# Cross attention: the scores of each head's last 16 rows on eight TensorE tiles instead of four

## The chip, the cores and the metric

The kernel runs on one core of a Trainium2 chip. The metric is the time of one execution on the device in microseconds; lower is better. TensorE does the matmuls and writes PSUM, ScalarE (ACT) and VectorE (DVE) read PSUM and work on SBUF, GpSimd (POOL) works on SBUF, and SyncE (SP) issues most DMAs.

## The reference

Sixteen sequences of 100 rows and 640 columns (`hidden_states`) attend to 718 context rows of 384 columns, with 8 heads of 80. A second, small attention by way of four more tokens is added. All in float32. The part that matters here is the first attention's scores:

```python
query = hidden_states @ Wq                     # 16 x 100 x 640
keyt = enc @ Wk                                # 16 x 718 x 640
valt = enc @ Wv
hs = _mha(query, keyt, valt)                   # softmax(q k^T / sqrt(80)) v, 8 heads of 80
...                                            # ca_hs2: the attention by way of the tokens
out = (hs + ca_hs2) @ Wout + b_out + residual
```

## The kernel before

The loop over the 16 batches is unrolled, and within it each engine's instructions run in the order in which the program issues them (a manual schedule). A batch `b` goes through these steps on TensorE: the scores of its queries against its keys in three groups (`scores(b, 0)`, `scores(b, 1)`, `scores(b, 2)`, L593), the products of the second attention (L823, L771), the values of this batch and the keys of the next in turns (L433 and L464), the last keys (L558), sometimes an output projection (L1048) or queries (L534), and then the weighted sums of the values (`a_ps`, L1453), after which the next batch begins with its scores.

The 718 keys are cut in six blocks of 120 or 119 (`KN` = 120). A group of scores takes two of them (`a` = 0, 1). Scores stand transposed: keys on the partitions, the 800 rows of the 8 heads along the free dimension, in four PSUM banks `s_ps[0..3]`, each with two heads' rows for both key blocks. A head has 80 columns, and so 80 rows of contraction, which don't fit into 64 partitions. They are cut into the first 64 and the last 16:

- `first_rows` (L618) contracts the first 64. Two heads lie above one another in 128 partitions, so there are two row groups of 64 partitions, and the 120 keys are cut into column tiles of 64 and 56 by `KH = [(0, 64), (64, KN)]` (L69). The moving operand is one head's 100 rows. A group of scores has 32 such products.
- `last_rows` (L637) contracts the last 16. All eight heads' last rows lie together in one chunk of 128 partitions (`kT[:, 4]`), two heads to 32 partitions. `qz` holds the queries for it, masked so that each of the two heads meets only its own 16: the moving operand is 200 elements, the 100 rows of the one head and then of the other. There are four row groups of 32 partitions (`RG` = 4), each writes a bank of its own, and each takes all 120 keys in one product. A group of scores has 8 such products.

Both write through the helper `product` (L605), so that all have line L608 in the profile; they are told apart by their inputs, `qp` and `qz`, and by their shapes. `product` adds to what the bank holds, and begins anew the first time that a quadrant of 32 partitions of a bank is written. Group 1 runs `last_rows` ahead of `first_rows`, groups 0 and 2 the other way round, so that the steps of groups 0 and 1 and those of groups 1 and 2 that have the same tiles lie next to each other:

```python
        steps = (last_rows, first_rows) if g == 1 else (first_rows, last_rows)
```

After a group, ScalarE copies the four banks to SBUF (L664 for groups 0 and 2, two banks at a time; L658 for group 1). Groups 0 and 2 use the same banks (`pair`), group 1 others.

Of the kernel before, what the change touches and what calls it, by code (L numbers as in the profile page):

```python
# [14 lines left out]
B, S, H = 16, 100, 640  # L15
# [8 lines left out]
KN = KT // 2  # L24
# [44 lines left out]
KH = [(0, 64), (64, KN)]  # L69
# [57 lines left out]
def kernel(  # L127
# [33 lines left out]
    def pair(name):  # L161
        tile = ps2.tile([P, 2, 512], F32, tag="ps2", name=name)
        return tile
# [21 lines left out]
    def scores_tile(name):  # L185
        return main.tile([P, 2, ROWS], F32, tag="st", name=name, bufs=NP)
# [28 lines left out]
    def load_enc(b):  # L215
        enc = enc_tile(f"enc_{b}"), None
        for u, lo, hi in ((0, 0, 3), (1, 1, 3), (2, 0, 2)):
            at = A_RAW[u, lo]
            nc.sync.dma_start(
                out=enc[0][:, at : at + hi - lo],  # L220
                in_=enct[b][:, lo:hi, u * (KT - 1) : u * (KT - 1) + KT],
            )
        return enc

    def load_rest(b, enc):
        if b == 1:
            room = hsT_tile("rest_1").rearrange("p c s -> p (c s)")
            rest = room[:, : len(A_REST) * KT].rearrange("p (i k) -> p i k", k=KT)
        else:
            rest = rest_tile(f"rest_{b}")  # L230
        for (u, c), i in A_REST.items():
            nc.sync.dma_start(
                out=rest[:, i], in_=enct[b][:, c, u * (KT - 1) : u * (KT - 1) + KT]
            )
        return enc[0], rest
# [19 lines left out]
    kT = const.tile([P, HC, 3, KT], F32, name="kT")  # L255
# [337 lines left out]
    def scores(b, g, tiles):  # L593

        qp, qz = tiles
        name = f"s_ps_{b}_{g}"
        if g == 1:
            s_ps = [f(f"{name}_{r}") for r, f in enumerate((psumk, psumk, psum1, psum1))]
        else:
            pairs = [pair(f"{name}_{i}") for i in range(2)]  # L600
            s_ps = [pairs[r // 2][:, r % 2] for r in range(RG)]
        n = KN
        begun = set()

        def product(at, part, w, rhs, cols, last):  # L605

            k0, k1 = part
            nc.tensor.matmul(  # L608
                s_ps[at][k0:k1, cols],
                w,  # L610
                rhs,
                start=not begun & {(at, k) for k in range(k0, k1, 32)},
                stop=last,
                skip_group_check=True,
            )
            begun.update((at, k) for k in range(k0, k1, 32))

        def first_rows(last):  # L618

            for a in range(2):  # L620
                u, j = KC[2 * g + a]
                for c in range(RG):
                    rhs = qp[:, c // 2, c % 2, (b % 2) * S : (b % 2 + 1) * S]
                    for r in range(2):
                        h, rows = RG * r + c, slice(64 * r, 64 * r + 64)
                        lo = 256 * a + (h % 2) * S
                        for k0, k1 in KH:
                            product(
                                h // 2,
                                (k0, k1),  # L630
                                kT[rows, c, u, j * KN + k0 : j * KN + k1],
                                rhs[rows],
                                slice(lo, lo + S),
                                last,
                            )

        def last_rows(last):  # L637

            for a in range(2):
                u, j = KC[2 * g + a]  # L640
                for r in range(RG):
                    rows = slice(32 * r, 32 * r + 32)
                    product(
                        r,
                        (0, n),
                        kT[rows, 4, u, j * KN : (j + 1) * KN],
                        qz[rows, 0, b % 2],
                        slice(256 * a, 256 * a + 2 * S),
                        last,
                    )  # L650

        steps = (last_rows, first_rows) if g == 1 else (first_rows, last_rows)
        for i, step in enumerate(steps):
            step(i == 1)
        st = scores_tile(f"st_{b}_{g}")[:n]
        if g == 1:
            for r in range(RG):
                nc.scalar.copy(  # L658
                    st[:, :, 2 * r * S : 2 * (r + 1) * S],
                    s_ps[r][:n].rearrange("p (a q) -> p a q", a=2)[:, :, : 2 * S],  # L660
                )
        else:
            for i in range(2):
                nc.scalar.copy(  # L664
                    st[:, :, 4 * i * S : 4 * (i + 1) * S].rearrange(
                        "p a (r q) -> p r a q", r=2
                    ),
                    pairs[i][:n].rearrange("p r (a q) -> p r a q", a=2)[:, :, :, : 2 * S],
                )
        return st  # L670
# [554 lines left out]
    last, enc_next, second_next = None, load_rest(1, load_enc(1)), Second(1, xT)  # L1225
# [8 lines left out]
    for b in range(B):  # L1234
# [243 lines left out]
        last = mine  # L1478
# [55 lines left out]
```

## Time and profile before

| what | value |
|---|---|
| median of the runs | 926.78 us (925.39 to 928.07, 3 runs) |
| profiled execution | 925.19 us |
| span of its instructions | 923.5 us |
| TensorE busy | 916.1 us, 99% of the span |
| VectorE, GpSimd, ScalarE busy | 687.4, 685.2, 434.0 us |
| granted TensorE clock | 0.999 |
| scores (L608), share of the chain that ended last | 11% |

A line of a group's view reads: line, engine, operation, tiles out<-in, shape, number of records, then the time in which at least one of them ran, the mean duration of one, and the idle time of the engine ahead of them. A shape such as `32*120 32x200` is 32 rows by 120 columns of the array and a moving operand of 32 partitions by 200 elements. PE is the matmuls, PEld the loads of the stationary operand into the array. An f32 product shows as two records of each.

### The profile page before, as it was taken

How to read it: one execution, taken by the hardware profiler on the slowest of the kernel's cores; microseconds unless marked ns; L12 is line 12 of the kernel's file. 1: busy time of each engine (PE TensorE's matmuls, PEld its weight loads, DVE VectorE, ACT ScalarE, POOL GpSimd, SP SyncE). 2: the span in 40 equal slices, each digit the busy share in tenths (PEclk: the TensorE clock that was granted, in tenths of full speed). 3: DMA queues.
4: the chain of work that ended last, by engine and by line, in shares of the span. 5: the costliest groups of instructions: out<-in, count | busy, mean ns of one | idle time of the engine just before them, and what ended most of it. 6: DMA issues, size and time to landing. Idle time of an engine off the chain costs nothing.

```text
span 923.5 us, 25899 instructions
## 1 busy us (share of the span) xinstructions
PE 916.1 (99%) x11130; PEld 773.0 (84%) x11130; DVE 687.4 (74%) x1085; ACT 434.0 (47%) x836; POOL 685.2 (74%) x646
## 2 busy tenths in 40 slices
PE   9999999999999999999999999999999999999998
PEld 6987889788797879888798887988879888797866
DVE  3459895988738897795867869579783898838883
ACT  2234543737327463552636526264641737427341
POOL 5757999688947888497784968758996589956723
PEclk9999999999999999999999999999999999999999
DMA  8822013050300404031030311205031050310201
GB/s 263 266 85 78 25 49 93 2 156 2 103 31 13 116 2 132 3 99 59 19 114 3 111 46 30 76 2 155 2 92 41 2 155 2 103 45 2 82 20 40
DMA packets 49673, 62.82 MB, mean 68 GB/s; under 512 B 14072, under 2 KB 38200, under 8 KB 49560
## 3 DMA queue, kind: packets, MB, share of 16 engines
q1 hardware_dynamic: 45512, 51.49, 18.1%
q0 software_dynamic: 3024, 8.53, 3.0%
q8 instruction: 87, 1.43, 0.6%
q10 hardware_dynamic: 1024, 1.15, 0.4%
q14 instruction: 26, 0.21, 0.1%
HBM read 55.59 MB, written 5.57 MB: 66 GB/s over the span
## 4 chain that ended last, share of the span: by engine, by line
PE 96%; DVE 2%; DMA 0%; issue 0%; ACT 0%; POOL 0%; ACTq 0%; DVEq 0%
PE a_ps L1453 12%; PE s_ps L608 11%; PE v_psA L433 11%; PE v_psB L433 9%; PE kT_ps L558 8%; PE k_psA L464 8%; PE q_ps L534 7%; PE k_psB L464 6%; PE o_ps L1048 5%; PE v_psC L433 3%; PE k_psC L464 3%; PE v_psD L433 2%; PE v_psE L433 2%; PE y_ps L771 2%; PE v_ps L374 1%; PE k_psE L464 1%
## 5 line engine op out<-in xcount | busy, mean ns | idle before, releaser
L796 POOL TENSOR_TENSOR e<-ca,g 100x800 f32<-100x800 f32 x64 | 97.9, 1540 | 115.5 <-PE v_psB L433 101.5
L499 POOL TENSOR_TENSOR enc<-enc 128x240 f32<-128x240 f32 x135 | 111.0, 832 | 16.5 <-DMA enc<-in_enct 9.4
L1256 DVE TENSOR_TENSOR st<-st,over 120x1600 f32<-120x1600 f32 x48 | 118.1, 2463 | 0.0
L1453 PEld LDWEIGHTS a_ps<-vs,st 120*36 120x36 f32 (+3 forms) x3072 | 109.2, 125 | 4.9 <-issue 4.8
L1453 PE MATMUL a_ps<-vs,st 120*36 120x81 f32 (+3 forms) x3072 | 112.0, 233 | 0.0
L433 PE MATMUL v_psA<-wv_sb,enc 128*120 128x320 f32 x352 | 109.8, 434 | 0.0
L897 POOL TENSOR_TENSOR hs<-hs,hs 100x640 f32<-100x640 f32 x48 | 102.0, 2125 | 3.8
L664 ACT COPY st<-s_ps 120x800 f32<-120x800 f32 x64 | 49.7, 829 | 98.7 <-PE s_ps L608 98.7
L803 POOL TENSOR_TENSOR e<-e,e 100x800 f32<-100x800 f32 x48 | 92.7, 1932 | 3.8
L890 POOL TENSOR_TENSOR hs<-vb,p 100x640 f32<-100x640 f32 x64 | 87.9, 1383 | 9.4 <-issue 4.8
L433 PE MATMUL v_psB<-wv_sb,enc 128*120 128x320 f32 x296 | 91.8, 433 | 0.0
L1264 ACT ACTIVATE st<-st 120x1600 f32<-120x1600 f32 x48 | 73.8, 1538 | 33.5 <-DVE st L1256 33.4
L464 PE MATMUL k_psA<-enc,wk_sb 128*128 128x240 f32 x360 | 87.8, 367 | 1.1 <-DVE kT L404 1.1
L464 PEld LDWEIGHTS k_psA<-enc,wk_sb 128*128 128x128 f32 x360 | 68.2, 190 | 18.4 <-POOL e L796 1.6
L1268 DVE TENSOR_TENSOR most<-most,st 120x800 f32<-120x800 f32 x64 | 71.2, 1113 | 15.6 <-ACT st L658 14.4
L433 PEld LDWEIGHTS v_psA<-wv_sb,enc 128*120 128x120 f32 x352 | 63.2, 183 | 22.6 <-issue 0.5
L464 PE MATMUL k_psB<-enc,wk_sb 128*128 128x240 f32 x300 | 73.1, 366 | 0.3 <-DVE sm L873 0.3
L608 PE MATMUL s_ps<-qp,kT 64*56 64x100 f32 (+1 forms) x3072 | 73.1, 248 | 0.0
L433 PEld LDWEIGHTS v_psB<-wv_sb,enc 128*120 128x120 f32 x296 | 54.1, 183 | 21.9 <-DVE vs L404 0.4
L608 PEld LDWEIGHTS s_ps<-qp,kT 64*56 64x56 f32 (+1 forms) x3072 | 66.9, 130 | 5.6 <-issue 4.2
L963 ACT COPY hsT<-turned_hs 32x160 f32<-32x160 f32 (+7 forms) x244 | 67.7, 278 | 3.0
L534 PE MATMUL q_ps<-xT,wq_sb 128*128 128x200 f32 x400 | 69.1, 333 | 0.0
(168 smaller groups left out, 1789.3 us busy)
## 6 DMA issues: line engine op xcount, KB each, us to landing
vb<-va_d POOLq DMA_DIRECT2D x32, 250.0 KB, 3.7
vb<-va_d SPq DMA_DIRECT2D x32, 250.0 KB
enc<-in_enct SPq DMA_DIRECT2D x30, 240.0 KB
enc<-in_enct SPq DMA_DIRECT2D x15, 360.0 KB
xT<-in_xt SPq DMA_DIRECT2D x8, 500.0 KB
rest<-in_enct SPq DMA_DIRECT2D x31, 120.0 KB
xn<-in_x SPq DMA_DIRECT2D x11, 320.0 KB
out<-xn SPq DMA_DIRECT2D x11, 320.0 KB
```

The source lines that it names most:

```text
L433: nc.tensor.matmul(at[0][j][:KN, : H // 2], a_form(self.enc, f)[:, j * KN : (j + 1) * KN], wv_there.get(f, wv_sb[:, W_AT[f]]), start=first ...
L464: nc.tensor.matmul(at[:, i * KT : (i + 1) * KT], wk_sb[:, W_AT[f], i], a_form(self.enc, f), start=(first and i == 0), stop=last, skip_grou ...
L499: nc.gpsimd.tensor_tensor(out, left, right, op)
L534: nc.tensor.matmul(q_ps[:, : 2 * S].rearrange("p (j s) -> p j s", j=2), wq_sb[:, c, n * P : (n + 1) * P], xT[:, :, c, :], start=(c == 0), ...
L558: nc.tensor.matmul(bank[:, i * KT : (i + 1) * KT], weights[c], a_raw(enc, u, c), start=(i == 0 and c == 0), stop=(c == CC - 1), skip_group ...
L608: nc.tensor.matmul(s_ps[at][k0:k1, cols], w, rhs, start=not begun & {(at, k) for k in range(k0, k1, 32)}, stop=last, skip_group_check=True,)
L796: first = nc.gpsimd.tensor_tensor(to, self.ca[:, t, :].unsqueeze(1).to_broadcast([S, NH, S]), g[:, :, t].unsqueeze(2).to_broadcast([S, NH, ...
L803: nc.gpsimd.tensor_tensor(e, e, to, ALU.add)
L890: first = nc.gpsimd.tensor_tensor(to, self.vb[t][:S].rearrange("p (h d) -> p h d", h=NH), p2[:, :, t].unsqueeze(2).to_broadcast([S, NH, D] ...
L897: nc.gpsimd.tensor_tensor(sums, sums, to, ALU.add)
L1256: return nc.vector.tensor_tensor(st[i], st[i], top.over[:KN].unsqueeze(1).to_broadcast([KN, 2, ROWS]), ALU.subtract,)
L1453: nc.tensor.matmul(a_v[lo:hi, h % 4], st[i // 2][: KEYS[i], i % 2, h * S + lo : h * S + hi], block(i, h // 4)[: KEYS[i], h % 4], start=(i ...
```

## The change

The products of `last_rows` are cut in two by the keys, in the same way as those of `first_rows`: the stationary operand is 64 keys and then 56 instead of 120, and each half writes its own half of the partitions of the same bank. The moving operand (200 elements), the row groups, the banks and the order of the steps stay.

```diff
                 for r in range(RG):
                     rows = slice(32 * r, 32 * r + 32)
-                    product(
-                        r,
-                        (0, n),
-                        kT[rows, 4, u, j * KN : (j + 1) * KN],
-                        qz[rows, 0, b % 2],
-                        slice(256 * a, 256 * a + 2 * S),
-                        last,
-                    )
+                    for k0, k1 in KH:
+                        product(
+                            r,
+                            (k0, k1),
+                            kT[rows, 4, u, j * KN + k0 : j * KN + k1],
+                            qz[rows, 0, b % 2],
+                            slice(256 * a, 256 * a + 2 * S),
+                            last,
+                        )
```

## The prediction

> **What bounds the kernel now.** I read the page first (busy shares, the clock, the chain that ended last), then the groups by shape for TensorE, then the time line of one batch's scores, and last some narrow slices of that time line, to see how a run of small tiles begins. From the page:
>
> ```profile
> span 923.5 us, 25899 instructions
> PE 916.1 (99%) x11130; PEld 773.0 (84%) x11130; DVE 687.4 (74%) x1085; ACT 434.0 (47%) x836; POOL 685.2 (74%) x646
> PEclk9999999999999999999999999999999999999999
> ...
> q8 instruction: 87, 1.43, 0.6%
> ...
> PE 96%; DVE 2%; DMA 0%; issue 0%; ACT 0%; POOL 0%; ACTq 0%; DVEq 0%
> PE a_ps L1453 12%; PE s_ps L608 11%; PE v_psA L433 11%; PE v_psB L433 9%; PE kT_ps L558 8%; PE k_psA L464 8%; PE q_ps L534 7%; PE k_psB L464 6%; PE o_ps L1048 5%; PE v_psC L433 3%; PE k_psC L464 3%; PE v_psD L433 2%; PE v_psE L433 2%; PE y_ps L771 2%; PE v_ps L374 1%; PE k_psE L464 1%
> ```
>
> The reader is to see that 96% of the last chain is TensorE, that its clock is granted in full throughout, and that the scores (L608, the line of the helper `product`) hold 11% of it. So a nanosecond taken from or put into TensorE's stream in the scores comes out of or goes into the span at full value; work moved on any other engine does not. The groups by shape split L608:
>
> ```profile
> L608 PE MATMUL s_ps<-qp,kT 64*64 64x100 f32 x1536 | 73.1, 248 | 0.0
> L608 PE MATMUL s_ps<-qp,kT 64*56 64x100 f32 x1536 | 72.9, 248 | 0.0
> L608 PE MATMUL s_ps<-qz,kT 32*120 32x200 f32 x768 | 41.3, 344 | 0.0
> ```
>
> The change rewrites the third row only. Three groups of scores in 16 batches have 2 x 4 x 3 x 16 = 384 products in `last_rows`, and the row counts 768: each f32 product is two records. The first two rows matter as much, because they are the nearest relative of what is coming: `first_rows` already splits its keys 64 and 56 onto two column tiles, over two row groups of 64. One batch on TensorE, column one the start, column two the length (ends are modelled; I use starts):
>
> ```profile
> 315.77 1.36 PE L1453 MATMUL a_ps<-vs,st 119*64 119x81 f32 x33
> 317.06 1.60 PE L608 MATMUL s_ps<-qp,kT 64*64 64x100 f32 x64
> 318.59 1.63 PE L608 MATMUL s_ps<-qz,kT 32*120 32x200 f32 x32
> 320.15 2.97 PE L608 MATMUL s_ps<-qp,kT 64*64 64x100 f32 x128
> 323.05 0.95 PE L608 MATMUL s_ps<-qz,kT 32*120 32x200 f32 x16
> 323.93 0.75 PE L823 MATMUL z_ps<-y_sb,e 100*32 100x33 f32 x64
> 324.61 0.61 PE L771 MATMUL y_ps<-m,xT 128*100 128x72 f32 x4
> ```
>
> There are two stretches of `last_rows` a batch: 32 records (groups 0 and 1 lie next to each other) and 16 records (group 2). Start to start they take 320.15 - 318.59 = 1.56 us and 323.93 - 323.05 = 0.88 us. The 16 records more cost 0.68 us, that is four rounds of four row groups at 0.170 us each; what is left, 0.88 - 0.68 = 0.20 us, is paid once a stretch. For `first_rows` the same: 1.53 us for 64 records, 2.90 us for 128, so 1.37 us for 16 rounds of four tiles, 0.0856 us each, and 1.53 - 1.37 = 0.16 us once.
>
> Two things follow. A round of twice the columns (200 against 100) takes 0.170 against 0.0856, so the part of a round that doesn't grow with the columns is about 2 x 0.0856 - 0.170 = 0.001 us: in both modes the rounds run at the speed at which the moving operand streams, and issue and weight loads are hidden behind it. And a row group with 120 columns and one with 64 stream at the same pace per element, so the array's width is no cost in the rounds.
>
> **The change part by part.**
>
> *The rounds.* Before, a batch has 48 records in 12 rounds of four. After, it has 96 records, each on half of the columns. If the two column tiles of a row group run side by side, these are 12 rounds of eight, each still 200 elements long: 12 x 0.170 us as before, a change of nothing. If they run in turn, each round is doubled. No row shows eight tiles at once, so I bound this: nothing from below (the moving operand of 200 elements still has to pass each row group, so a round can't be shorter), 0.170 us a round from above, 16 x 12 x 0.170 = 32.6 us in all. I take nothing, because the two rows nearest to it show the two halves: four row groups at once in `last_rows` now, two column tiles in each row group at once in `first_rows` (four tiles in 0.0856 us, of which one alone streams 100 elements).
>
> *The start of a stretch.* Slices of the time line just after the first records of each kind have ended, so that the first start shown is that of the second round:
>
> ```profile
> 318.69 0.20 PEld L608 LDWEIGHTS s_ps<-qz,kT 32*120 32x120 f32 x4
> 318.86 0.50 PE L608 MATMUL s_ps<-qz,kT 32*120 32x200 f32 x6
> 317.12 0.22 PEld L608 LDWEIGHTS s_ps<-qp,kT 64*64 64x64 f32 x6
> 317.20 0.42 PE L608 MATMUL s_ps<-qp,kT 64*64 64x100 f32 x10
> ```
>
> In `last_rows` the first load goes at 318.59 and the second at 318.69, 0.10 us later: the first 120 columns take that long to load. The second matmul follows at 318.86, 0.27 us after the first, which is 0.10 of load and 0.17 of round. In `first_rows` the second load comes 0.06 us after the first (317.06 to 317.12) and the second matmul 0.14 us after, 0.06 and 0.08. So the first load lies open once a stretch, and costs 0.10 us at 120 columns and 0.06 us at 64. Subtracted from the 0.20 and 0.16 above, both leave 0.10 us, the rows' order and the emptying of the array before the next mode. With column tiles of 64 the load term goes from 0.10 to 0.06: 0.04 us less a stretch.
>
> *The order of eight.* Against that stands the first issue of eight loads instead of four. All four first pairs are out within 0.03 us:
>
> ```profile
> 317.06:317.09 0.03, 0.03 (x4) 0.03 (x4) 1.00 0.00 0
> 318.59:318.62 0.03, 0.03 (x8) 0.03 (x4) 1.00 0.00 0
> ```
>
> (counts of matmuls and of weight loads in brackets; the second slice's matmul count holds four of the mode before). That is about 0.007 us a pair as an estimate, so the last of eight begins 4 x 0.007 = 0.03 us later than the last of four, and the stretch ends as much later. The bounds are nothing (if pairs of column tiles fall into step) and 0.04. The Trainium skill, "TensorE: Matmul & The Clock Gate", section "Measured speedup vs the span model", puts a pack of tiles at one matmul's time plus about 4 ns for each further tile; by that page the four tiles more would cost 0.016 us, and the sum would be nearer 0.8 us of gain than the one below. The trace's step here is the larger, and I go by it.
>
> *Sum.* 0.04 - 0.03 = 0.01 to 0.02 us saved a stretch, 32 stretches: 0.6 us, with bounds of 32 x 0.04 = 1.3 us of gain and nothing.
>
> *What else is issued.* 384 products more are 768 matmul records and 768 weight loads. Queue q8 brought 1.43 MB for 2 x 11130 TensorE records, 64 bytes each, so this is 0.1 MB more. The pace asked for is eight pairs in 0.170 us, 0.021 us a pair, the pace of `first_rows` (0.0856 / 4). The L823 row shows 64 pairs in 324.61 - 323.93 = 0.68 us, 0.011 us a pair with its start and end, so the issuer can go twice as fast. If that cover were gone, each 0.001 us a pair too slow would cost 1.5 us over the 1536 pairs that `last_rows` then has.
>
> *Who waits behind it.* ScalarE copies the banks out, and group 2 takes group 0's banks again:
>
> ```profile
> 319.63 1.56 ACT L664 COPY st<-s_ps 120x800 f32<-120x800 f32 x2 [3.37 <-PE s_ps L608]
> ACT st L664 <- PE s_ps L608: 98.7, 32, 7.9
> ```
>
> The copies of group 0 end at 319.63 + 1.56 = 321.19. TensorE comes to group 2 half way through the 2.90 us that begin at 320.15, near 321.6, so 0.4 us to spare; a shift of 0.02 us changes nothing. ScalarE waits 98.7 us for these scores already: it isn't the bound. No wait, transfer or queue position is added.
>
> The profiled execution took 925.19 us with a span of 923.5, so 1.7 us lie around it; by the sum it becomes 924.6. It is 1.6 us under the median of 926.78, inside the runs' spread of 925.39 to 928.07; the difference carried to the median gives 926.2 us.
>
> **The rivals.**
>
> *The column tiles take turns (slower).* The eight tiles share four row groups' streams, and if the second column tile of a row group is fed only when the first has had its 200 elements, a round is 0.340 us: 32.6 us more, 959 us. For it: nothing in the trace has eight tiles. Against it: `first_rows`' 0.0856 us a round. It turns the sign early: 0.3% is 2.8 us, about what a measurement of this kernel can tell from no change, and with the 0.6 us saved that is reached when a round grows by 3.4 / 192 = 0.018 us, a tenth.
>
> *The weight loads come into the open (slower).* With eight tiles each next load might not be pulled ahead of the matmul running in its row group. Then each of the 192 rounds pays the 0.06 us that now opens a stretch: 11.5 us, about 937.7 with the saving. Against it: in `first_rows` the second load starts at 317.12, before the second matmul at 317.20, and in rounds of 0.0856 us there is no room for 0.06 us in the open. This is what a rule of the Trainium skill would give ("TensorE: Matmul & The Clock Gate", section "The mechanism": a weight load overlaps matmuls in flight only where the row group differs). The trace disagrees with it for tiles that differ in columns alone.
>
> *The mode change becomes free (faster).* 64 columns wide on both sides, the 32-row and 64-row stretches might pass into each other without emptying the array. Three such borders a batch at 0.10 us are 4.8 us: about 921.4. Against it: the border from L1453 to L608. L1453's matmuls also stand on column tiles of 64 and less, and its last one, 0.234 us long by its group, starts at 315.77 + 1.36 - 0.234 = 316.90; L608 follows at 317.06, 0.16 us later:
>
> ```profile
> L1453 PE MATMUL a_ps<-vs,st 120*64 120x81 f32 x1024 | 102.4, 234 | 0.0
> 373.09 6.87 PE s_ps L608 x146
> ```
>
> The array empties there too, although only the rows change. (The second row is from the chain of waits of another batch: its 6.87 us, the same as 1.53 + 1.56 + 2.90 + 0.88 = 6.87 here, shows that one batch stands for all.)
>
> *It doesn't do what it says.* The shapes 64*56 in the groups show that tiles of 56 columns at column 64 are built as asked; I give this no chance of its own.
>
> **How the numbers follow.** Eight tiles at once, 926.2 us: 0.70. Its own range is 924.9 to 927.5, the bounds of nothing and 1.3 us with some 0.7 us for a median of few runs. Column tiles in turn, 959 us: 0.13. Loads in the open, 937.7 us, or part of it: 0.10. Free mode change, 921.4 us or part of it: 0.07. The range reaches from 924.0 to 938.0: it takes in the first and the third, 0.80, and leaves out the other two, 0.20. Within 0.3%: 0.70; slower: 0.13 + 0.10 = 0.23; faster: 0.07.
>
> **What would show it.** In the changed profile: L608 with rows 32*64 and 32*56, 768 records each, their matmuls as long as now (328 ns in steady rounds); the two stretches at 1.54 and 0.86 us start to start, a second weight load 0.06 us after the first; chain and page otherwise unchanged, TensorE still 99%. Stretches of some 2.9 us and 1.6 us would show column tiles in turn; 2.0 and 1.1 us the open loads; a start of the next mode less than 0.1 us after the last round the free change. I am wrong if any of these appear, or if the other lines of TensorE move.

## The result and the profile after

The change makes the kernel slower: 943.04 us (942.35 to 944.07, 4 runs) against 926.31 us, a ratio of 1.0176 with a 95% interval of 1.0162 to 1.0191. That is 16.7 us more where 0.6 us less was forecast, and outside the range. The profiled execution took 942.35 us. From the page of the changed kernel, the lines that answer to those shown of before:

```profile
span 940.6 us, 27435 instructions
...
PE 922.9 (98%) x11898; PEld 775.1 (82%) x11898; DVE 684.1 (73%) x1085; ACT 434.7 (46%) x836; POOL 679.8 (72%) x646
...
q8 instruction: 93, 1.52, 0.7%
...
PE 97%; issue 1%; DVE 1%; DMA 0%; POOL 0%; ACTq 0%; DVEq 0%
```

The span grew by 17.1 us, TensorE's busy time by 6.8 only. "issue" in the chain has gone from 0% to 1%: time in which an engine waited for nothing that the profile shows. The time line of TensorE says where. First the first batch (start, length, both in us), then the fourth, which begins at 204.70:

```profile
60.36 1.60 PE L608 MATMUL s_ps<-qp,kT 64*64 64x100 f32 x64
61.89 1.60 PE L608 MATMUL s_ps<-qz,kT 32*64 32x200 f32 x64
63.42 3.34 PE L608 MATMUL s_ps<-qp,kT 64*64 64x100 f32 x128
66.69 0.93 PE L608 MATMUL s_ps<-qz,kT 32*64 32x200 f32 x32
67.54 0.65 PE L824 MATMUL z_ps<-y_sb,e 100*32 100x33 f32 x53
...
204.70 1.60 PE L608 MATMUL s_ps<-qp,kT 64*64 64x100 f32 x62
207.31 0.38 PE L608 MATMUL s_ps<-qp,kT 64*56 64x100 f32 x2 [1.01 <-issue]
207.61 1.72 PE L608 MATMUL s_ps<-qz,kT 32*64 32x200 f32 x64
209.27 1.58 PE L608 MATMUL s_ps<-qp,kT 64*64 64x100 f32 x61
211.15 1.75 PE L608 MATMUL s_ps<-qp,kT 64*64 64x100 f32 x67 [0.29 <-issue]
212.83 0.93 PE L608 MATMUL s_ps<-qz,kT 32*64 32x200 f32 x32
213.69 0.45 PE L824 MATMUL z_ps<-y_sb,e 100*32 100x33 f32 x28
214.97 0.48 PE L824 MATMUL z_ps<-y_sb,e 100*32 100x33 f32 x36 [0.84 <-issue]
215.38 1.12 PE L772 MATMUL y_ps<-m,xT 128*100 128x72 f32 x10
```

In the first batch the eight tiles do what the prediction had them do: 63.42 - 61.89 = 1.53 us for the long stretch (1.56 before) and 67.54 - 66.69 = 0.85 us for the short one (0.88). Twice the records, no more time. But the 64-row tiles between them, which the change leaves alone, already take 66.69 - 63.42 = 3.27 us where they took 2.90.

In the fourth batch TensorE stops three times. Count the records between the stops, over all tile shapes: 2 + 64 + 61 = 127 from the first to the second, 67 + 32 + 28 = 127 from the second to the third. The stops don't follow a step or a tile shape; two lie among the 64-row tiles that the change doesn't touch, one in L824. They follow a count of instructions: each f32 record is a weight load and a matmul, so about 256 instructions lie between stops.

The whole trace bears this out. Number TensorE's records (matmuls, weight loads and its sequencer's own) from the start of the program: the weight loads in the scores, L824 and L772 waited longer than 0.31 us 16 times since the first batch's scores, each time at a record whose number leaves 194, 195 or 196 when divided by 256, and nowhere else. The kernel before has no such wait there. Queue q8 moved 1.52 MB in 93 transfers, 16 KB each, and 16 KB is 256 instructions of the 64 bytes worked out before. The DMA view of the window from 204.6 to 217 us, in 40 slices, holds the transfers themselves:

```profile
GB/s 61 0 0 0 0 0 0 0 0 0 0 0 53 0 0 0 0 0 0 0 0 0 0 0 0 0 53 0 0 0 0 0 0 0 0 0 0 53 0 0
...
q8 instruction: 4, 0.07, 2.3%
```

One block every 11 to 14 slices of 0.31 us, 3.8 us on average, with the DMA engines idle between: nothing competes with it. The four transfers took 2.3% of 16 engines' 12.4 us, 1.1 us each; what the rest of the 3.8 us goes to, no view shows. Over all batches, from the starts of each stretch, the steps from the first score to L772 take 16.9 us longer than before: the undisturbed stretches are shorter by 0.05 us a batch, 0.8 us in all, and 17.7 us of stops come on top.

### The profile page after: what moved, and what is told of

The parts are those of the page before. It is cut to its first block, busy times and chain, and to the rows that moved or that the text cites. A ratio compares the mean times of both kernels' runs of the same rounds, so it can differ in the third digit from the quotient of the medians.

```text
span 940.6 us, 27435 instructions
## 1 busy us (share of the span) xinstructions
PE 922.9 (98%) x11898; PEld 775.1 (82%) x11898; DVE 684.1 (73%) x1085; ACT 434.7 (46%) x836; POOL 679.8 (72%) x646
## 3 DMA queue, kind: packets, MB, share of 16 engines
q8 instruction: 93, 1.52, 0.7%
## 4 chain that ended last, share of the span: by engine, by line
PE 97%; issue 1%; DVE 1%; DMA 0%; POOL 0%; ACTq 0%; DVEq 0%
PE s_ps L608 12%; PE a_ps L1454 12%; PE v_psA L433 10%; PE v_psB L433 9%; PE kT_ps L558 8%; PE k_psA L464 8%; PE q_ps L534 7%; PE k_psB L464 6%; PE o_ps L1049 5%; PE v_psC L433 3%; PE k_psC L464 3%; PE y_ps L772 2%; PE v_psD L433 2%; PE v_psE L433 2%; PE v_ps L374 2%
## 5 line engine op out<-in xcount | busy, mean ns | idle before, releaser
L499 POOL TENSOR_TENSOR enc<-enc 128x240 f32<-128x240 f32 x135 | 104.5, 784 | 16.3 <-DMA enc<-in_enct 9.3
L1257 DVE TENSOR_TENSOR st<-st,over 120x1600 f32<-120x1600 f32 x48 | 114.9, 2394 | 0.0
L898 POOL TENSOR_TENSOR hs<-hs,hs 100x640 f32<-100x640 f32 x48 | 104.9, 2186 | 3.8
L891 POOL TENSOR_TENSOR hs<-vb,p 100x640 f32<-100x640 f32 x64 | 85.1, 1340 | 9.8 <-issue 4.7
L1269 DVE TENSOR_TENSOR most<-most,st 120x800 f32<-120x800 f32 x64 | 69.1, 1079 | 19.8 <-ACT st L659 18.7
L608 PE MATMUL s_ps<-qp,kT 64*56 64x100 f32 (+1 forms) x3072 | 76.8, 249 | 3.4 <-issue 3.4
L608 PEld LDWEIGHTS s_ps<-qp,kT 64*56 64x56 f32 (+1 forms) x3072 | 68.6, 130 | 11.8 <-issue 10.3
```

Of the source, the lines that this page charges most:

```text
L499: nc.gpsimd.tensor_tensor(out, left, right, op)
L608: nc.tensor.matmul(s_ps[at][k0:k1, cols], w, rhs, start=not begun & {(at, k) for k in range(k0, k1, 32)}, stop=last, skip_group_check=True,)
L891: first = nc.gpsimd.tensor_tensor(to, self.vb[t][:S].rearrange("p (h d) -> p h d", h=NH), p2[:, :, t].unsqueeze(2).to_broadcast([S, NH, D] ...
L898: nc.gpsimd.tensor_tensor(sums, sums, to, ALU.add)
L1257: return nc.vector.tensor_tensor(st[i], st[i], top.over[:KN].unsqueeze(1).to_broadcast([KN, 2, ROWS]), ALU.subtract,)
```

## The experiments

Two theories. A, supply: TensorE's instructions come in blocks of some 128 pairs, one in 3.7 or 3.8 us, so about 0.029 us a pair (a pair is a record's weight load and its matmul); where small tiles consume a pair in 0.021 us, the run lives on what was in hand and then stops at each border of a block. B, tiles: eight tiles at once disturb each other or the matmuls next to them.

**1. The same count without column tiles.** `last_rows` of the kernel before, cut in two by the moving operand:

```diff
-                    product(r, (0, n), ..., qz[rows, 0, b % 2], slice(256 * a, 256 * a + 2 * S), last)
+                    for s0 in (0, S):
+                        product(r, (0, n), ..., qz[rows, 0, b % 2, s0 : s0 + S],
+                                slice(256 * a + s0, 256 * a + s0 + S), last)
```

> The kernel before, but each product of last_rows is cut in two by the moving operand (100 and 100 elements) instead of by the keys: 120 columns and four row groups as before, no column tiles, and the same 96 records a batch as the change. A round of four then streams 100 elements in 0.086 us while its 120 columns need 0.10 us to load, so the rounds alone should cost 24 x 0.10 - 12 x 0.17 = 0.4 us a batch, some 6 us in all. Theory A (TensorE's instructions come in blocks of about 127 pairs, a block every 3.8 us or so, and the run of small tiles empties what is in hand): stalls of 0.3 to 1.2 us, 127 or 128 pairs apart, as in the changed kernel, and some 10 us beside the 6: 941 to 944 us. Theory B (eight tiles at once get in each other's way): no such stalls, 932 to 933 us.

Measured: 944.8 us, ratio 1.0193 (1.0159 to 1.0226). The time line has the stops, here 16 + 112 = 128 records apart, with four tiles of 120 columns and none of 64 in `last_rows`:

```profile
776.95 1.36 PE L608 MATMUL s_ps<-qz,kT 32*120 32x100 f32 x38
778.51 0.70 PE L608 MATMUL s_ps<-qz,kT 32*120 32x100 f32 x16 [0.20 <-issue]
779.15 2.63 PE L608 MATMUL s_ps<-qp,kT 64*64 64x100 f32 x112
782.26 0.57 PE L608 MATMUL s_ps<-qp,kT 64*64 64x100 f32 x16 [0.48 <-issue]
```

The total is 0.8 us above A's range, and its parts are not A's: the undisturbed stretches cost 12.4 us more (0.78 us a batch, where 0.4 was expected, since a round of 100 elements behind loads of 120 columns takes 0.123 us and not 0.10), the stops 7.8 us. Slower rounds leave supply more time, so this too goes A's way. By B there would be no stops here.

**2 and 3. As many pairs fewer elsewhere.** The products behind the scores (L823, L824) with one tile of 100 columns a head instead of four, in both kernels:

```diff
-                for lo, hi in QZ:
+                for lo, hi in [(0, S)]:
```

> The kernel before, but the products at L823 take a head's 100 columns as one tile instead of four tiles of 32, 32, 32 and 4: 16 records a batch instead of 64, each with a load of about 0.083 us in place of rounds of 0.035. Both theories: no stalls beyond those of before, 16 x 0.083 = 1.33 against 0.55 us a batch, some 12 us more: 936 to 941 us. It is the reference for the next one.

> The changed kernel with the same edit at L824: 48 pairs a batch fewer in the run of small tiles, as many as the change adds, and eight tiles in last_rows as in the change. Theory A: the run is as long as before the change, stalls nearly vanish, and the time is that of the kernel before with the same edit less the 0.7 us that shorter first loads save, within 3 us of it. Theory B: the stalls belong to the eight tiles and stay, 14 to 17 us over the kernel before with the same edit.

Measured: 935.82 us (1.0100, 1.0072 to 1.0128) without the change, just under the range expected, and 946.29 us (1.0215, 1.0186 to 1.0244) with it: 10.5 us apart. Neither theory's number. The waits for weight loads, without and with the change (total us, times, longest), show where it went:

```profile
PEld s_ps L608 <- issue: 4.2, 17, 0.2
PEld z_ps L823 <- issue: 3.4, 14, 0.2
```

```profile
PEld s_ps L608 <- issue: 9.7, 27, 0.7
...
PEld z_ps L824 <- issue: 4.8, 17, 0.3
```

(4.2 and 3.4 are the mode changes, and the same in the kernel before.) The stops behind the scores are nearly gone: 0.2 us over all batches, from the starts of the stretches, against 7.1 us in the changed kernel. Those inside the scores stayed, 9.3 us against 10.6 (both with the 0.12 us a batch that is told further down). My use of A was wrong: I counted the pairs of the whole run, but a stop comes as soon as the pairs issued so far outrun supply, and the pairs saved here come after the scores. The scores alone were 240 pairs in 6.87 us, 0.0286 each, just at the pace of supply; now they are 288 in 6.82, 0.0237 each.

**4. Supply measured by itself.** The kernel before, the products at L823 issued six times over:

```diff
-            for h in range(NH):
+            for h in [*range(NH)] * 6:
```

> The kernel before, with the products at L823 issued six times over (each overwrites the last, so the output stays): 384 pairs of four column tiles in a row instead of 64, no eight tiles anywhere. Theory A: the run goes at the pace of supply, about 3.8 us for 127 pairs or 0.030 us a pair, in bursts of 0.009 us a pair with stalls 127 pairs apart; some 9 to 10 us a batch more, 1060 to 1090 us in all. Theory B: 0.009 to 0.011 us a pair throughout, 3 us a batch more, 970 to 985 us.

Measured: 1099.13 us in 2 runs, 1.1862 (1.1805 to 1.1919). One batch of it:

```profile
183.73 1.08 PE L823 MATMUL z_ps<-y_sb,e 100*32 100x33 f32 x102
186.55 1.29 PE L823 MATMUL z_ps<-y_sb,e 100*4 100x33 f32 x128 [1.74 <-issue]
190.28 1.99 PE L823 MATMUL z_ps<-y_sb,e 100*4 100x33 f32 x128 [2.44 <-issue]
194.01 0.60 PE L823 MATMUL z_ps<-y_sb,e 100*4 100x33 f32 x26 [1.74 <-issue]
```

This is the price: 128 records, then a stop; 190.28 - 186.55 = 3.73 and 194.01 - 190.28 = 3.73 us a block, 0.029 us a pair, though the tiles of one block took 1.29 us and those of the next 1.99. Over this run, 26 blocks lie between two such stops; they took 3.5 to 4.6 us, the median being 3.73. No eight tiles are in it. From the first score to L771 a batch takes 9.3 us more than before, as A had it, but the total came out 9 us over A's range. TensorE's mean granted clock was 0.939 here, where the other runs have 0.998 or more: 1.00 from 186.55 to 187.70 us and 0.50 from 190.28 to 192.20. The products behind these stops took twice their time for a while, ten of L771 1.79 us instead of 0.96, which I had not counted.

**5 and 6. Part of the change.** In the changed kernel:

```diff
-                    for k0, k1 in KH:
+                    for k0, k1 in KH if g == 2 else [(0, n)]:   # the other run: g < 2
```

> The change in group 2 alone: last_rows of groups 0 and 1 stay at 120 columns, so a batch has 16 pairs more than before, not 48. Theory A (supply of instructions, with the price read from the runs so far: a block of 128 pairs every 3.8 us, 0.0297 us a pair, against a run of 320 pairs that streams in 7.52 us, less 1.2 to 1.8 us that is in hand when the run begins): 9.50 - 7.52 = 1.98 us short, 0.2 to 0.8 us of stalls a batch, 3 to 12 us in all, and nearly all of it in the products behind the scores, since the scores alone (256 pairs in 6.84 us) need 7.60: 929 to 938 us. Theory B (a fixed price of eight tiles): a third of the change's 16.7 us, 931 to 932 us, with the loss in group 2's own stretch.

> The change in groups 0 and 1 alone: 32 pairs a batch more. Theory A: 336 pairs, 9.98 us of supply against 7.52 us of streaming, 0.7 to 1.2 us of stalls a batch, 936 to 945 us, in part inside the scores. Theory B: two thirds of 16.7 us, 937 us, all in the stretch of groups 0 and 1.

Measured: group 2 alone 933.56 us (1.0074, 1.0058 to 1.0089), groups 0 and 1 alone 939.17 us (1.0136, 1.0118 to 1.0155). So 16, 32 and 48 pairs more cost 7.3, 12.9 and 16.7 us. Both times lie in A's ranges, which were wide; B's numbers, 5.6 and 11.1 us, lie inside the 95% intervals (5.4 to 8.2 and 10.9 to 14.4 us), so the times don't decide between the two. The place does. With group 2 alone the fourth batch reads:

```profile
204.72 0.91 PE L608 MATMUL s_ps<-qp,kT 64*64 64x100 f32 x30
205.96 1.06 PE L608 MATMUL s_ps<-qp,kT 64*56 64x100 f32 x34 [0.32 <-issue]
206.95 1.63 PE L608 MATMUL s_ps<-qz,kT 32*120 32x200 f32 x32
208.51 2.97 PE L608 MATMUL s_ps<-qp,kT 64*64 64x100 f32 x128
211.41 0.93 PE L608 MATMUL s_ps<-qz,kT 32*64 32x200 f32 x32
212.27 0.45 PE L824 MATMUL z_ps<-y_sb,e 100*32 100x33 f32 x28
212.98 0.23 PE L824 MATMUL z_ps<-y_sb,e 100*32 100x33 f32 x3 [0.27 <-issue]
```

Group 2's own stretch is undisturbed, 212.27 - 211.41 = 0.86 us; the stops lie ahead of it and behind it. Over all batches they are 4.4 us behind the scores and 2.6 us in group 0's first tiles, where B wanted them in group 2's stretch. With groups 0 and 1 alone, 6.3 us are in the 64-row tiles of groups 1 and 2, 3.7 us behind the scores and 2.5 us in the stretch of eight tiles, where B wanted all of them. A is off here too: it had nearly all of group 2's loss behind the scores, and the stops in group 0 come before any record that this edit adds to the batch. Where a block's border falls is set by all instructions since the program's start: in all runs of this document that have waits of more than 0.31 us in the scores, in the products behind them (L823 or L824) or in L772, 115 in all, their numbers divided by 256 leave 194, 195 or 196, as in the changed kernel.

**7 and 8. The same instructions, another order.** The next batch's first two key products, slow ones, ahead of the fast ones behind the scores, in both kernels (the edit abridged):

```diff
         st.append(scores(b, 2, tiles))
+        kk = None
+        if 0 < b < B - 1:
+            kk = Keys(b + 1, enc)
+            kk.go(2)
         now.softmax2()
 ...
-            both(3)
+            vv.go(3)
+            kk.go(1)
```

> The kernel before, but the next batch's first two key products (8 pairs of 0.2 us) are issued between group 2's scores and the products at L823, instead of some microseconds later. Same instructions, another order. Both theories: no change to speak of, 924 to 929 us, unless the later start of the second attention delays GpSimd. It is the reference for the next one.

> The changed kernel with the same move: eight tiles, all 96 records, every instruction kept, but 1.6 us of slow products ahead of the 64 fast pairs that follow the scores. Theory A: supply catches up by 1.6 / 0.0297 = 54 pairs there; the stalls at the products behind the scores (7.4 us in the changed kernel, and 1 us behind them) nearly vanish, those inside the scores stay: 933 to 937 us. Theory B: nothing but the place has changed, 943 us.

Measured: 934.44 us (1.0091, 1.0068 to 1.0114) without the change, 942.86 us (1.0174, 1.0155 to 1.0192) with it. The move costs 8 us by itself, which I had not expected: a later key product now waits 7.7 us in all for ScalarE to free its bank.

```profile
PEld k_psD L464 <- ACT vs L406: 7.7, 14, 0.6
```

Against that reference the change costs 8.4 us, half of 16.7. In the changed kernel with the move the fourth batch runs through L824 without a stop:

```profile
212.29 1.08 PE L464 MATMUL k_psA<-enc,wk_sb 128*128 128x240 f32 x4
213.21 0.97 PE L464 MATMUL k_psB<-enc,wk_sb 128*128 128x240 f32 x4
214.11 0.75 PE L824 MATMUL z_ps<-y_sb,e 100*32 100x33 f32 x64
214.79 0.40 PE L772 MATMUL y_ps<-m,xT 128*100 128x72 f32 x2
```

214.79 - 214.11 = 0.68 us, the kernel before's time, where the change needs 215.38 - 213.69 = 1.69 us. Eight slow pairs ahead of them, 214.11 - 212.29 = 1.82 us, were enough. Over all batches L824 takes 0.9 us more than in its reference, nearly all of it in the last batch, which the move leaves as it was, against 7.1 us more in the change without the move; the stops inside the scores, which come ahead of the move, stay. A's absolute range (933 to 937) is missed by the price of the move, its difference isn't; B's 943 is met only because the price of the move makes up for what the stops gave back: against the reference B has 16.7 us, which the 8.4 refute.

No version is faster than the kernel before. All that eight tiles can bring is the 0.8 us of shorter first loads, and no order tried here gives supply the time for them.

## Why the prediction was wrong

*The rounds and the start of a stretch:* right. Eight tiles of 32 by 64 stream at once; the rival in which they take turns and the one with loads in the open are refuted by the first batch, 1.53 and 0.85 us against 2.9 and 1.6, or 2.0 and 1.1. The sum of 0.6 us saved came out as 0.8. That a tile's width costs nothing in the rounds holds for 200 elements; for 100 elements behind loads of 120 columns a round took 0.123 us (run 1).

*The mode change:* not free, as forecast; the undisturbed stretches fit the same emptying as before.

*What else is issued:* this step failed. I took q8's row, worked out 64 bytes an instruction and 0.1 MB more, and stopped there, with the term at nothing. It measured 17.7 us. The cover that I named was L823 with 0.011 us a pair. But that is a burst of 64 pairs, half a block, out of what is in hand, and says nothing of the pace that lasts. A warning was to be had from the same row: 16 KB a transfer is 128 pairs, and a pair in 0.021 us asks for one in 2.7 us. In the kernel before, the DMA view from 203.8 to 213 us, a batch's scores, has two transfers 16 slices of 0.23 us apart, 3.7 us:

```profile
GB/s 0 0 0 0 0 0 0 0 0 0 0 0 0 71 0 0 0 0 0 0 0 0 0 0 0 0 0 0 0 71 0 0 0 0 0 0 0 0 0 0
...
q8 instruction: 2, 0.03, 1.3%
```

That supply could not go faster, no view of the kernel before shows; it took the runs. The sentence on its price, 1.5 us for each 0.001 us a pair too slow, shows the size that was at stake: at 0.029 us a pair for supply and 0.021 for the tiles it is 12 us, of the order of what came. I gave it neither a bound nor a rival; none of the three rivals is what happened. 937.7 us in the range was the nearest, by another mechanism.

The Trainium skill, "Runtime: NRT & Kernel Launch", section "Instruction fetch mechanics", says that an engine's instructions arrive in blocks of 256, the next while the current one executes, and that crossing a border is mostly hidden. The trace agrees with the first (127 or 128 records of two instructions between stops, 16 KB a transfer) and not, for this stream of small tiles, with the second (17.7 us of stops).

*Who waits behind it:* right; other engines have no more of the chain than before. In 15 of 16 batches the long stretch also takes 0.12 us more than in the first one (three of them have a stop on top), as in this batch without any stop, 383.26 - 381.61 = 1.65 us:

```profile
381.61 1.72 PE L608 MATMUL s_ps<-qz,kT 32*64 32x200 f32 x64
383.26 2.97 PE L608 MATMUL s_ps<-qp,kT 64*64 64x100 f32 x128
```

and, from the answer for line L608 (minimum, median and longest in ns):

```profile
L608 PEldq EVENT_SEMAPHORE  x38: 51/51/51, 98.4 to 891.8; - x38
```

TensorE's sequencer has two semaphore records of 51 ns in that stretch, and the first batch has none. In the kernel before, the stretch takes 1.56 us with and without them. That they are waits for group 1's banks, and that they show now because the same lead in instructions is half the time with smaller tiles, is argued, not shown: a kernel without them wasn't tried. It is 1.8 us of the 17.7.

Open is how much is in hand at the start of a run. The runs fit 1.2 to 1.8 us of streaming beyond supply, an estimate (a batch's pairs from the first score to L772 times 0.029 us, less their streaming, less their stops), and where in a block the run begins moves it.

## What to carry to other kernels

Cutting matmuls into more tiles that run side by side cost no streaming time here, but it cost instructions, and TensorE's instructions had a pace of their own. Before such a cut, count the pairs in a run of small tiles, divide by its time, and compare with what a long run of the same core sustains, not with a short burst. Where they are close, ask what the run has used up before the place in question, not only its total. Stops that keep an equal number of instructions apart, across lines and shapes, were supply here, and are a reason to look at the instruction queue.

## What the runs showed of the hardware that I had not expected

TensorE's instruction stream sustained 128 pairs of weight load and matmul in 3.73 us (the median), 0.029 us a pair, with idle DMA engines, while bursts went at 0.010 to 0.011 (128 pairs within 1.29 us in run 4, 64 in 0.68 us at L823). The kernel before stands at this edge: its scores take 0.0286 us a pair and it shows next to no stops, and 16 pairs a batch more already cost 7.3 us. Eight f32 tiles, four of 32 rows by 64 columns and four of 32 by 56, streamed at once at the full pace of each: 64 records in 1.53 us where 32 wider ones took 1.56.
